# Turning the experts' rows with DMA transposes of 16-bit halves in place of TensorE transposes

## The chip, the core and the metric

The kernel runs on one core of a Trainium2 chip. A core has a matrix engine (TensorE, PE in the profile), a vector engine (VectorE, DVE), a scalar engine (ScalarE, ACT), a general engine (GpSimd, POOL) and an engine that only issues transfers (SyncE, SP). Each works through its own queue of instructions in order and waits for the others by semaphores. Transfers run on 16 DMA engines; they are issued from SP's queue (plain transfers here) or GpSimd's (those with a list of row indices). Tensors lie in SBUF with 128 partitions; TensorE writes to PSUM[...]. The metric is the time of one execution on the device, in microseconds (us), less being better.

## The reference, cut to what matters

```python
x = x + L0_xattn(layernorm(x), ctx)      # correlation of sequences, top 12 shifts
x = x + L0_ffn(layernorm(x))             # 8 experts, 256 tokens each
x = x + L1_xattn(layernorm(x), ctx)      # 16-head attention
x = x + L1_ffn(layernorm(x))

def L1_ffn(h):                           # h: 2048 tokens x 256
    probs = softmax(h @ gate_W.T)        # 8 experts, each token goes to its best two
    gates = top2(probs)
    y_e = (silu(h @ w1[e]) * (h @ w3[e])) @ w2[e]          # 256 -> 1024 -> 256
    shared = mean over 8 narrow shared experts of the same form
    return 0.5 * shared + 0.5 * sum_e gates[:, e] * y_e
```

Everything is in float32. The change lies in the last part, the mixture of experts of the second layer. Its 8 narrow shared experts are handled as one of width 1024, so that it has the size of a routed expert.

## The kernel before, in words

The order of every engine's work is the order of the program: `tc.manual_schedule` (line 1256) leaves each engine's instructions as they are written. What follows from 395 us on is the expert stage.

*Routing.* Each token's row (256 values, 8 gates and its token number, 265 in all) lies in the tile HP. GpSimd scatters the rows, 128 at a time, into a table Td in HBM in which every expert has its own stretch of rows (`send`, line 2887; 32 transfers, each waiting for the one before, the last at 427.14 us). The first 512 rows of an expert are handled in its block; the few beyond that go to "slots" of 32 rows, worked on beside blocks 2 to 6 (`slots`, line 3598), with their own weight loads (`load_slots`) from SP's queue.

*Blocks.* The loop over b (line 3796) has 11 blocks of 512 rows: 0 and 1 are the shared expert on the second and third quarter of the tokens, 2 to 9 are the routed experts 0 to 7, 10 is the shared expert on the last quarter. Block b first runs the up unit (b, 0), then the down unit of block b - 1, then the up units (b, 1) to (b, 3). An up unit computes two 128-wide stretches of the hidden layer; a down unit maps all 1024 back to 256.

*Units.* Each unit is a 2 x 2 block product by seven multiplications (Winograd's form). Its operands are quarters and their sums, the sums being made beforehand by DVE: of the weights (`UpWeights.steps`, `DownWeights.steps`), of the rows (`Rows.steps`, which writes tile T and one quarter of the rows in place) and of the activations (`act_sums`). `run_unit` (line 3407) writes out the order: the seven products, reads of PSUM by ACT and DVE between them, and the end of the unit before (`end_open`), whose gate products and sums DVE makes then. It takes lists of further work to be put at four places, called early, amid, late and after. A down unit's products read the four act tiles of its block in the order 0, 1, 2, 3.

*Rows of an expert.* `load_rows` (line 3489) asks on SP for 512 rows from Td, into the one buffer R. TensorE needs them with the 256 features on the partitions: `Turned.half` turns four 128 x 128 squares into one PSUM bank and ACT copies them into RT (two buffers). Half 0 runs early and half 1 amid the down unit of block b, for the rows of block b + 1; for expert 0 both run in unit (1, 3). Two small DVE copies take the token numbers (ids) and gates (gts) out of R. Then DVE makes the sums T, late in the same down unit.

*Results.* A routed down unit scales its rows by the gates and GpSimd adds them, in four transfers of 128 rows, to the rows of the output Od in HBM (`add_rows`, line 3517). Each of the four waits until the one before has landed. The slots add four small ones of their own.

*Space.* HP is no longer needed once it is sent, and its first 3072 of 4240 elements per partition hold the sums of the up weights (SW, line 3758). Of X, the first six of 16 tiles hold the sums of the down weights from block 2 on (TW); the last four (lrows) are stored to Od ahead of the stage and come back in the last block.

Of the kernel before, what the change touches and what calls it, by code (L numbers as in the profile page):

```python
# [9 lines left out]
F32 = mybir.dt.float32  # L10
BF16 = mybir.dt.bfloat16
U32 = mybir.dt.uint32
I32 = mybir.dt.int32
AF = mybir.ActivationFunctionType
ALU = mybir.AluOpType
# [4 lines left out]
P = 128  # L20
LN_EPS = 1e-5
CAP1 = 576
FIRST = 512
# [1063 lines left out]
def fast_path(  # L1087
# [33 lines left out]
    nc = tc.nc  # L1121
    B, S, D = x.shape
    T = B * S
    NT = T // P
    KC = D // P
    TPB = S // P
    E = L0_ffn_w1.shape[0]
# [22 lines left out]
    X = res.tile([P, NT, D], F32, name="X")  # L1150
# [3 lines left out]
    ROW = D + E + 1  # L1154
# [13 lines left out]
    ident = const.tile([P, P], F32, name="ident")  # L1168
# [93 lines left out]
    pm = l0.enter_context(tc.tile_pool(name="pm", bufs=2))  # L1262
# [34 lines left out]
    for dst, src, i in (  # L1297
# [12 lines left out]
        out=bqd.rearrange("o (b c) -> (o b) c", b=B),  # L1310
        in_=L0_xattn_bq.partition_broadcast(B),
    )
    nc.scalar.dma_start(
        out=WZ[:, :, DH : 2 * DH],
        in_=L0_xattn_Wq.rearrange("(kc p) c -> p kc c", p=P),
# [267 lines left out]
    for h in range(TPB):  # L1583
# [36 lines left out]
        out=tri,  # L1620
        in_=tri,
# [26 lines left out]
    for sign, base in ((1, 1), (-1, 16)):  # L1648
        nc.gpsimd.affine_select(
            out=rows_f,  # L1650
            in_=rows_f,
# [33 lines left out]
    for r in range(2):  # L1685
        (nc.sync if r == 0 else nc.scalar).dma_start(
            out=Gd[0, 0 : S * W2].rearrange(
                "(tt p r w) -> p tt r w", p=P, r=2, w=S
            )[:, :, r, :],
            in_=G,  # L1690
# [4 lines left out]
        out=DG,  # L1695
        in_=Gd[0, :].rearrange("(tt p w) -> p tt w", p=P, w=W2 + 1)[:, :, 1 : S + 1],
# [53 lines left out]
    for tt in range(2):  # L1750
# [3 lines left out]
    rest = pa.tile([P, S], F32, name="rest")  # L1754
# [4 lines left out]
        out=rest, in_to_replace=top[:, 0, :], in_values=pcorr, imm_value=-3.0e38  # L1759
# [16 lines left out]
        out=Wd[:, 0:W2].rearrange("o (r s) -> o r s", r=2),  # L1776
        in_=wrow.unsqueeze(1).to_broadcast([P, 2, S]),
# [4 lines left out]
        out=CW,  # L1782
        in_=bass.AP(wd.tensor, wd.offset + P - 1, [[WD - 1, P], [P, 2], [1, S]]),
# [186 lines left out]
    sums = pa.tile([P, NT, 2], F32, name="sums")  # L1970
# [50 lines left out]
    halves = [slice(m * S, (m + 1) * S) for m in range(2)]  # L2021
# [7 lines left out]
    b = order_b  # L2029
# [101 lines left out]
    def load_row(e):  # L2131
# [14 lines left out]
        out=Yd.rearrange("(c p) d -> p c d", p=P),  # L2146
        in_=blank[:, 0:D].unsqueeze(1).to_broadcast([P, NT, D]),
# [300 lines left out]
    for e in range(E - 1):  # L2448
        if e == 5:

            wpv = L1_xattn_Wp.rearrange("(c g m d) n -> m g d c n", c=NB, g=4, m=2)
            for m in range(2):
                for g in range(4):
# [3 lines left out]
                        out=bvc[r0 : r0 + DH, :],  # L2457
                        in_=bkv[:, 1, :].rearrange("(c g m) d -> m g d c", c=NB, g=4)[m, g],
# [70 lines left out]
    ps_m = banks.enter_context(tc.tile_pool(name="ps_m", bufs=3, space=PSUM))  # L2529
# [436 lines left out]
    for b in range(B):  # L2966
        for c in range(NB):
# [55 lines left out]
            if prev is None:  # L3023
# [12 lines left out]
                HP = pg1.tile([P, NT, ROW], F32, name="HP")  # L3036
# [20 lines left out]
    FULL = FIRST // P  # L3057
# [7 lines left out]
    lrows = slice(LAST * (TB // P), NT)  # L3065
    HT2 = TB // 2
    HF = F // 2
# [17 lines left out]
    class UpWeights:  # L3085


        def __init__(self, wab, sums, s1=None):
            self.sums = sums
            self.raw = {  # L3090
                (h, kc): wab[:, :, kc, h * HF : (h + 1) * HF]
                for h in range(2)
                for kc in range(KC)
            }
            self.part = {
                A11: self.raw[0, 0],
                A12: self.raw[0, 1],
                A22: self.raw[1, 1],
                S1: self.raw[1, 0] if s1 is None else s1,
                S3: sums[:, :, 0],  # L3100
                S2: sums[:, :, 1],
                S4: sums[:, :, 2],
            }
# [120 lines left out]
    class Up(Unit):  # L3224
        n = TB
# [56 lines left out]
    class Down(Unit):  # L3282
        n = HT2
# [123 lines left out]
    def run_unit(u, early=(), amid=(), late=(), after=()):  # L3407

        before = open_unit[0]
        u.mm(u.a, A11, "b11", True)  # L3410
        u.seed()
        if before is not None:
            before.silu_2()
        u.mm(u.e, S1, "t1", True)
        u.read_p5()
        end_open()
        for do in early:
            do()
        u.mm(u.a, S2, "t2")
        u.read_u2()  # L3420
        u.mm(u.b, A12, "b21")
        for do in amid:
            do()
        u.mm(u.e, S4, "b22")
        u.read_c12()
        for do in late:
            do()
        u.mm(u.a, S3, "t3")
        u.read_c22()
        for do in after:  # L3430
            do()
        open_unit[0] = u
# [56 lines left out]
    def load_rows(e):  # L3489
        R = pe2.tile([P, FULL, ROW], F32, tag="R", name="R", bufs=1)  # L3490
        nc.sync.dma_start(
            out=R,
            in_=Td[e * CAP1 : e * CAP1 + FIRST, :].rearrange("(r p) w -> p r w", p=P),
        )
        return R

    class Turned:


        def __init__(self, e, R):  # L3500
            self.e, self.R = e, R
            self.RT = pe2.tile([P, KC, FIRST], F32, tag="RT", name="RT")
            self.ids = pe2.tile([P, FULL], U32, tag="ids", name="ids", bufs=3)
            self.gates = pe2.tile([P, FULL], F32, tag="gts", name="gts", bufs=3)

        def half(self, kc):
            pt = ps_m.tile([P, FULL, P], F32, tag="pm", name="pt")
            for r in range(FULL):
                nc.tensor.transpose(
                    pt[:, r, :], self.R[:, r, kc * P : (kc + 1) * P], ident  # L3510
                )
            nc.scalar.copy(self.RT[:, kc, :], pt.rearrange("p r q -> p (r q)"))
            if kc == 0:
                nc.vector.tensor_copy(self.ids, self.R[:, :, ROW - 1])
                nc.vector.tensor_copy(self.gates, self.R[:, :, D + self.e])

    def add_rows(Y, ids):
        nc.gpsimd.indirect_dma_start(  # L3518
# [164 lines left out]
    pe2 = ctx.enter_context(tc.tile_pool(name="pe2", bufs=2))  # L3683
# [63 lines left out]
    ps_m = ctx.enter_context(tc.tile_pool(name="ps_m", bufs=1, space=PSUM))  # L3747
# [20 lines left out]
    ups, downs, xs_, acts, Rs = {0: shared, 1: shared}, {}, {}, {}, {}  # L3768
    downs[0] = downs[1] = shared_down
    xs_[0], xs_[1], xs_[NBLK - 1] = rows[1], rows[2], rows[LAST]  # L3770
    turned = {}

    def up_unit(b, k):
        u = Up(ups[b], xs_[b], k, acts.setdefault(b, []))
        u.with_sums = b < NBLK - 1
        return u
# [19 lines left out]
    for b in range(NBLK):  # L3796


        n = b + 1
        rest = ups[b].steps(P, HF) if b >= 2 else []  # L3800
        run_unit(up_unit(b, 0), after=rest[:2])
        if b == 0:
            Rs[2] = load_rows(0)
        if b >= 2 and b - 1 < E:
            W_up[b - 1] = load_up(w1p, b - 1)
        halves = []
        if 2 <= n < NBLK - 1:
            t = turned[n] = Turned(n - 2, Rs.pop(n))
            xs_[n] = Rows(t.RT)
            halves = [lambda: t.half(0), lambda: t.half(1)]  # L3810
        sums = xs_[n].steps() if n < NBLK else []
        if b > 0:
            late = b == 1
            run_unit(
                down_unit(b - 1),
                early=([] if late else halves[:1]) + rest[2:],
                amid=[] if late else halves[1:],
                late=[] if late else sums,
            )
        if 2 <= b < E:  # L3820
            Rs[b + 2] = load_rows(b)
        for k in range(1, NK):
            early, amid, after = [], [], []
            if k == 1 and 2 <= n < NBLK:
                ups[n] = UpWeights(WS[0] if n == NBLK - 1 else W_up.pop(n - 2), SW)
                after = ups[n].steps(0, P)
            if 2 <= b < NBLK - 1:
                if k == 2:
                    downs[b] = DownWeights(W_down.pop(b - 2), TW)
                    after = downs[b].steps()[:2]  # L3830
                if k == 3:
                    after = downs[b].steps()[2:]
            if b == 0:
                after = ([assign_slots], sums, shared_down.steps())[k - 1]
            if b == 1 and k == 3:
                early, amid, after = halves[:1], halves[1:], sums
            run_unit(up_unit(b, k), early, amid, after=after)
            if k == 1:
                if b >= 2 and b - 1 < E:
                    W_down[b - 1] = load_down(w1p, b - 1)  # L3840
                if b == 1:
                    flags()
                    experts = slot_experts()
                if b == 2:
                    beside = slots()
                if b == NBLK - 1:
                    nc.sync.dma_start(out=X[:, lrows, :], in_=odv[:, lrows, :])
                    nc.sync.dma_start(
                        out=out.rearrange("b s d -> (b s) d")[0 : LAST * TB, :],
                        in_=Od[0 : LAST * TB, :],  # L3850
                    )
            if beside is not None and (b, k) != (2, 2):
                next(beside, None)
        if b == 1:
            Rs[3] = load_rows(1)
    last_down(WS[1], acts.pop(NBLK - 1))
    order.close()

# [51 lines left out]
```

## Time and profile before

| | |
|---|---|
| median of 3 runs | 831.76 us (830.33 to 832.37) |
| the profiled execution | 830.43 us, its span 828.7 us |
| granted TensorE clock | 0.998 |
| TensorE busy | 806.3 us, 97% of the span |
| DVE, ACT, GpSimd busy | 522.3, 348.7 and 216.8 us |
| DMA | 105.4 MB; engines busy 35.0% by SP's and 7.2% by GpSimd's queue |
| a block with slots / without | 41.0 / 37.6 us |

The profile is of one execution. Rows give the line, engine, operation and tiles (out<-in), their count and durations; a timeline gives start and duration in microseconds from the span's start; "idle before" names what an engine waited for. The durations of matmuls overlap in their pipeline, so that the distance of their starts, not their durations, tells what they cost. Where an engine waits for several things, the profile names the one that came last by its own reckoning.

### The profile page before, as it was taken

The page shows a single profiled execution, that of the slowest core. Times are in us where ns is not written, and L with a number is a line of the kernel's source. Part 1 is how long each engine was busy: PE and PEld are TensorE (multiplying, and loading weights), DVE is VectorE, ACT ScalarE, POOL GpSimd, SP SyncE. Part 2 cuts the span into 40 slices and gives each one's busy share as a digit, 9 for nine tenths or more (in the row PEclk, how much of TensorE's full clock was granted, in tenths as well). Part 3 has the DMA queues.
Part 4 walks back from the last instruction along what each step waited for, and adds up shares of the span by engine and source line. Part 5 has one row for each costly group of instructions (what it writes and reads, how often), then busy time and mean ns, then how long its engine had stood idle before and what let it go on. Part 6 is the DMA issues. An engine that isn't in the chain of part 4 may idle for free.

```text
span 828.7 us, 13872 instructions
## 1 busy us (share of the span) xinstructions
PE 806.3 (97%) x5188; PEld 636.2 (77%) x5188; DVE 522.3 (63%) x1470; ACT 348.7 (42%) x720; POOL 216.8 (26%) x293
## 2 busy tenths in 40 slices
PE   7999999999999999999999999999999999999997
PEld 6546787778745555557898989797979798999996
DVE  6377877440456586555775866767676758586731
ACT  4344454324377777431333233333333433443430
POOL 6251131230125455452330000202111232112020
PEclk9999999999999999999999999999999999999999
DMA  8395567942160000042120474656575754311023
GB/s 261 97 277 177 178 207 224 297 158 84 51 178 15 14 1 28 34 168 89 67 67 26 142 242 135 190 168 187 172 199 161 201 167 122 105 13 20 8 35 124
DMA packets 87316, 105.40 MB, mean 127 GB/s; under 512 B 9000, under 2 KB 77832, under 8 KB 87208
## 3 DMA queue, kind: packets, MB, share of 16 engines
q1 hardware_dynamic: 78568, 91.10, 35.0%
q0 software_dynamic: 7920, 13.02, 7.2%
q8 instruction: 43, 0.70, 0.4%
q10 hardware_dynamic: 752, 0.30, 0.1%
q14 instruction: 33, 0.27, 0.1%
HBM read 80.61 MB, written 25.37 MB: 128 GB/s over the span
## 4 chain that ended last, share of the span: by engine, by line
PE 88%; DMA 5%; DVE 3%; POOL 2%; ACT 1%; issue 1%; ACTq 0%; SPq 0%; DVEq 0%; POOLq 0%
PE a L3234 18%; PE e L3234 9%; PE a L3293 9%; PE py L2389 6%; PE ph L2372 5%; PE B L3234 5%; PE e L3293 4%; PE p L2652 4%; PE py L3439 3%; PE pv L2667 3%; PE B L3293 2%; PE pp L2718 2%; DMA R<-NMd,ids 2%; PE pgt L3196 2%; PE pp L2619 2%; PE pu L3196 2%
## 5 line engine op out<-in xcount | busy, mean ns | idle before, releaser
L3518 POOL DMA_INDIRECT Od<-Y,ids x32 | 51.6, 1612 | 300.5 <-DVE T L3083 184.0
L3222 ACT COPY B<-a 128x512 f32<-128x512 f32 (+1 forms) x54 | 28.6, 531 | 180.5 <-PE a L3234 142.6
L2660 ACT ACTIVATE ex<-p,scale 128x512 f32<-128x512 f32 x128 | 77.2, 689 | 27.5 <-PE p L2652 26.3
L3234 PE MATMUL a<-T,HP 128*128 128x256 f32 x288 | 73.9, 379 | 0.0
L3083 DVE TENSOR_TENSOR cc<-e,s 128x512 f32<-128x512 f32 x44 | 30.4, 691 | 58.0 <-PE e L3234 58.0
L3234 PE MATMUL a<-RT,wab 128*128 128x256 f32 x256 | 66.6, 383 | 0.0
L3083 DVE TENSOR_TENSOR act<-act 128x256 f32<-128x256 f32 (+1 forms) x120 | 61.4, 512 | 2.7
L2372 PE MATMUL ph<-RT,w 128*128 128x256 f32 x256 | 61.7, 389 | 0.8 <-ACT RT L2359 0.7
L2389 PE MATMUL py<-w,A 128*128 128x256 f32 x256 | 61.6, 388 | 0.0
L3234 PEld LDWEIGHTS a<-T,HP 128*128 128x128 f32 x288 | 54.0, 190 | 7.0
L3234 PEld LDWEIGHTS a<-RT,wab 128*128 128x128 f32 x256 | 46.4, 190 | 8.4 <-issue 1.6
L2381 ACT ACTIVATE A<-ph,b1c 128x256 f32<-128x256 f32 x64 | 30.0, 472 | 53.9 <-PE ph L2372 50.6
L2372 PEld LDWEIGHTS ph<-RT,w 128*128 128x128 f32 x256 | 45.3, 190 | 8.9 <-ACT A L2381 1.1
L2389 PEld LDWEIGHTS py<-w,A 128*128 128x128 f32 x256 | 46.6, 190 | 6.4
L2892 POOL DMA_INDIRECT Td<-HP,to x32 | 32.9, 1030 | 56.9 <-DMA Td<-HP,to 51.6
L2652 PE MATMUL p<-QM,KT 32*128 32x512 f32 x256 | 43.4, 640 | 0.4 <-DVE QM L2633 0.4
L3083 DVE TENSOR_TENSOR act<-act,cc 128x512 f32<-128x512 f32 x44 | 30.4, 691 | 17.6 <-ACT act L3268 17.1
L2399 POOL DMA_INDIRECT Yd<-Y,ids x16 | 15.7, 984 | 81.9 <-DVE Y L2398 49.0
L2667 PE MATMUL pv<-ex,VA 128*32 128x256 f32 x512 | 34.5, 385 | 0.2 <-DVE ov L2677 0.2
L3249 ACT COPY s<-a 128x512 f32<-128x512 f32 x44 | 25.7, 585 | 20.4 <-PE a L3234 20.4
L2667 PEld LDWEIGHTS pv<-ex,VA 128*32 128x32 f32 x512 | 13.5, 109 | 27.0 <-issue 11.7
L3234 PE MATMUL e<-T,wab 128*128 128x256 f32 x128 | 33.0, 380 | 0.3 <-DVE T L3083 0.3
(525 smaller groups left out, 1745.0 us busy)
## 6 DMA issues: line engine op xcount, KB each, us to landing
w<-in_L_ffn_w_dram SPq DMA_DIRECT2D x16, 1024.0 KB, 6.0
wab<-in_L_ffn_w_e_dram SPq DMA_DIRECT2D x16, 1024.0 KB, 4.9
wc<-in_L_ffn_w_e_dram SPq DMA_DIRECT2D x8, 1024.0 KB, 5.4
sab<-in_L_ffn_w_e_dram SPq DMA_DIRECT2D x32, 256.0 KB, 2.9
R<-Td SPq DMA_DIRECT2D x8, 530.0 KB, 3.7
sc<-in_L_ffn_w_e_dram SPq DMA_DIRECT2D x16, 256.0 KB, 2.8
Td<-blank SPq DMA_DIRECT2D x2, 1590.0 KB, 10.2
X<-in_x_dram SPq DMA_DIRECT2D x4, 512.0 KB, 5.3
```

What stands on the lines that cost most here:

```text
L2372: nc.tensor.matmul(ph, w1[:, kc, f * P : (f + 1) * P], RT[:, kc, :], start=(kc == 0), stop=(kc == KC - 1),)
L2381: nc.scalar.activation(A[:, f, :], ph, AF.Gelu_apprx_tanh, bias=b1c[:, e, f : f + 1])
L2389: nc.tensor.matmul(py, A[:, f, r * P : (r + 1) * P], w2[:, f, :], start=(f == 0), stop=(f == NF - 1),)
L2652: nc.tensor.matmul(ps[g].rearrange("p m q -> p (m q)"), KT[rows, c, k0 : k0 + P], QM[b][rows, c].rearrange("p m q -> p (m q)"), start=True ...
L2660: nc.scalar.activation(e4[:, g], ps[g], AF.Exp, scale=scale)
L2667: nc.tensor.matmul(pvs[b, c][32 * g : 32 * g + 32, m, :], VA[:, b * TPB + kt, 8 * c + 2 * g + m, :], ex[b, c, kt][:, g, m, :], start=(kt = ...
L2892: nc.gpsimd.indirect_dma_start(out=Td, out_offset=bass.IndirectOffsetOnAxis(ap=to[g][:, k, j : j + 1], axis=0), in_=HP[:, GT * g + j, :], ...
L3083: eng.tensor_tensor(out, a, b, op)
L3196: nc.tensor.matmul(ps, wab[:, m, kc, fs], xs[kc], start=(kc == 0), stop=(kc == KC - 1),)
L3234: nc.tensor.matmul(ps[:, m * HT2 : (m + 1) * HT2], self.w.get(m, left, self.k), self.x.part[right], start=start and m == 0, stop=True, ski ...
L3293: nc.tensor.matmul(ps[:, qs], self.acts[k][:, left, qs], self.w.get(right, k), start=start and i == 0 and k == 0, stop=(k == NK - 1), skip ...
L3518: nc.gpsimd.indirect_dma_start(out=Od, out_offset=bass.IndirectOffsetOnAxis(ap=ids, axis=0), in_=Y, in_offset=None, compute_op=ALU.add,)
```

## The change

The transposes of the routed experts' rows leave TensorE. For the rows of an expert, GpSimd copies the 32-bit values out of R as 16-bit halves into the last four tiles of X, all low halves of a row before all high ones. Four DMA transposes from SP's queue, one for each 128 rows, turn them into a stretch of HP behind the weight sums. Two GpSimd copies (`join`) put the halves together into RT. ACT's copies from PSUM are gone too.

The places change with it. `Turned` (with the ids and gates, the split and the four transposes) now runs at the end of block b, after unit (b, 3), for the rows of block b + 2, from block 0 on. `join` runs in block b + 1, after its first up unit. The sums T stay where they were: late in the down unit, or after unit (1, 3) for expert 0. The load of R for block b + 2 is asked for in block b after the down unit, in block 1 too, where it was at the end of the block; for expert 0 it stays in block 0 after the first unit.

```diff
+U16 = mybir.dt.uint16
...
     class Turned:
         def __init__(self, e, R):
-            self.e, self.R = e, R
-            self.RT = pe2.tile([P, KC, FIRST], F32, tag="RT", name="RT")
             self.ids = pe2.tile([P, FULL], U32, tag="ids", name="ids", bufs=3)
             self.gates = pe2.tile([P, FULL], F32, tag="gts", name="gts", bufs=3)
-
-        def half(self, kc):
-            pt = ps_m.tile([P, FULL, P], F32, tag="pm", name="pt")
+            nc.vector.tensor_copy(self.ids, R[:, :, ROW - 1])
+            nc.vector.tensor_copy(self.gates, R[:, :, D + e])
+            parts = X[:, lrows, :].bitcast(U16).rearrange("p r (t d) -> p r t d", t=2)
+            nc.gpsimd.tensor_copy(
+                parts.rearrange("p r t d -> p r d t"),
+                R[:, :, 0:D].bitcast(U16).rearrange("p r (d t) -> p r d t", t=2),
+            )
+            self.turned = (
+                HP.rearrange("p n r -> p (n r)")[:, 2 * 3 * HF : 2 * 3 * HF + KC * FIRST]
+                .bitcast(U16)
+                .rearrange("p (c q) -> p c q", q=FIRST)
+            )
             for r in range(FULL):
-                nc.tensor.transpose(
-                    pt[:, r, :], self.R[:, r, kc * P : (kc + 1) * P], ident
-                )
-            nc.scalar.copy(self.RT[:, kc, :], pt.rearrange("p r q -> p (r q)"))
-            if kc == 0:
-                nc.vector.tensor_copy(self.ids, self.R[:, :, ROW - 1])
-                nc.vector.tensor_copy(self.gates, self.R[:, :, D + self.e])
+                nc.sync.dma_start_transpose(
+                    out=self.turned[:, :, r * P : (r + 1) * P],
+                    in_=parts[:, r].rearrange("p t d -> p (t d)"),
+                )
+
+        def join(self):
+            self.RT = pe2.tile([P, KC, FIRST], F32, tag="RT", name="RT")
+            for kc in range(KC):
+                nc.gpsimd.tensor_copy(
+                    self.RT[:, kc, :].bitcast(U16).rearrange("p (q t) -> p q t", t=2),
+                    self.turned[:, kc : kc + 3 : 2, :].rearrange("p t q -> p q t"),
+                )
+            return Rows(self.RT)
...
-        halves = []
         if 2 <= n < NBLK - 1:
-            t = turned[n] = Turned(n - 2, Rs.pop(n))
-            xs_[n] = Rows(t.RT)
-            halves = [lambda: t.half(0), lambda: t.half(1)]
+            xs_[n] = turned[n].join()
...
-                early=([] if late else halves[:1]) + rest[2:],
-                amid=[] if late else halves[1:],
+                early=rest[2:],
...
-        if 2 <= b < E:
+        if 1 <= b < E:
             Rs[b + 2] = load_rows(b)
...
             if b == 1 and k == 3:
-                early, amid, after = halves[:1], halves[1:], sums
-            run_unit(up_unit(b, k), early, amid, after=after)
+                after = sums
+            run_unit(up_unit(b, k), after=after)
+            if k == 3 and b < E:
+                turned[b + 2] = Turned(b, Rs.pop(b + 2))
...
-        if b == 1:
-            Rs[3] = load_rows(1)
```

More of the change, by code (lines that the diff above doesn't have):

```diff
@@ L3815, in fast_path @@
                 down_unit(b - 1),
-                early=([] if late else halves[:1]) + rest[2:],
-                amid=[] if late else halves[1:],
+                early=rest[2:],
                 late=[] if late else sums,
             )
-        if 2 <= b < E:
+        if 1 <= b < E:
             Rs[b + 2] = load_rows(b)
         for k in range(1, NK):
-            early, amid, after = [], [], []
+            after = []
             if k == 1 and 2 <= n < NBLK:
```

## The prediction

> **What bounds the kernel now.** I read the page's busy times and its chain first. TensorE works through 97% of the span, at a granted clock of 0.998 in the list of cores:
>
> ```profile
> PE 806.3 (97%) x5188; PEld 636.2 (77%) x5188; DVE 522.3 (63%) x1470; ACT 348.7 (42%) x720; POOL 216.8 (26%) x293
> PE 88%; DMA 5%; DVE 3%; POOL 2%; ACT 1%; issue 1%; ACTq 0%; SPq 0%; DVEq 0%; POOLq 0%
> ```
>
> Then the chain in order of time over the expert stage and the answer for tile R. The transposes are on the chain, four at a time:
>
> ```profile
> 452.69 0.44 PE pt L3509 x4
> 453.13 0.86 PE a L3234 x4
> ...
> 472.03 0.44 PE pt L3509 x4
> L3509 PE MATMUL pt<-ident,R x64: 272/273/273, 452.5 to 711.7; 128*128 128x128 f32 x64
> ```
>
> A transpose is recorded at 0.273 us, but four hold TensorE for 0.44 us. From 395.7 to 822 us TensorE waits for nothing worth naming (one 0.3 us wait for DVE at 458).
>
> Third, the timelines of SP, DVE and PE where the changed order first bites, and the waits of SP:
>
> ```profile
> 422.74 0.68 DVE L3083 TENSOR_TENSOR act<-act,cc 128x512 f32<-128x512 f32 x1
> 423.34 0.41 DVE L3083 TENSOR_TENSOR act<-act,B 128x256 f32<-128x256 f32 x1
> 425.32 1.95 PE L3293 MATMUL a<-wc_-1_2739,act 128*128 128x128 f32 x16
> 429.73 0.36 SPq L3491 DMA_DIRECT2D R<-Td  x1
> SPq L3491 <- DMA Td<-HP,to: 33.6, 1, 33.6
> GB/s 57 0 0 0 0 0 0 0 0 0 0 42 106 78 106 155 85 191 339 389 382 375 375 382 410 417 283 156 254 0 0 0 0 0 0 0 0 0 0 0
> ```
>
> The last line is the DMA view of 429 to 435 us in 40 slices of 0.15 us: R of the first expert, issued at 429.73 when the scatters to Td have landed, is in by 29 slices, at 433.4 us.
>
> Fourth, the deadline of a turned tile in a later block (period 41.0 us) and GpSimd's queue:
>
> ```profile
> 553.83 0.75 DVE L3083 TENSOR_TENSOR T<-RT 128x256 f32<-128x256 f32 x2
> 555.42 0.60 DVE L3362 SCALAR_TENSOR_TENSOR Y<-a,gts,Y 128x128 f32<-128x128 f32 x2
> 556.42 1.95 PE L3293 MATMUL a<-wc,act 128*128 128x128 f32 x16
> 572.83 1.55 POOL L3518 DMA_INDIRECT Od<-Y,ids  x1 [6.26 <-ACT act L3259]
> 673.69 1.85 POOL L3518 DMA_INDIRECT Od<-Ys,ids_s  x1 [1.69 <-DMA Od<-Ys,ids_s]
> 676.81 0.75 DVE L3083 TENSOR_TENSOR T<-RT 128x256 f32<-128x256 f32 x2
> L1597 POOL COPY WK<-wkv_in 128x512 f32<-128x512 f32 x1 | 0.7, 711 | 0.0
> L1561 POOL COPY rexp<-R 128x256 f32<-128x256 f32 x1 | 0.4, 393 | 0.1
> ```
>
> DVE's sums T wait for the turned rows, and behind them stands the read (L3362) that TensorE needs 0.4 us after its end (556.02 to 556.42). So T may start 0.4 us late; beyond that TensorE stops, microsecond for microsecond.
>
> [...] two DVE scalings beside a GpSimd addition took 2.39 us at 232.29 where such a pair takes 0.73 us; but DVE's two-input X<-X,yg kept its 0.68 us at 260.49 beside GpSimd's scaling, and that GpSimd pair took 2.73 us, 2.44 us where no such DVE operation ran.
>
> **The change, part by part.**
>
> *Removed:* 16 groups of four transposes, 16 x 0.44 = 7.0 us, all on the chain. The 16 ACT copies (L3512, 0.585 us each) go too, 9.4 us of an engine with 42%: nothing on the path.
>
> *Moved, first expert:* Turned now runs at the end of block b, two blocks ahead, and starts with two DVE copies from R (ids, gates). In block 0 they stand between the last sum of the shared down weights (ends 422.8) and the gating of unit (0,3) (422.74). R is in at 433.4. DVE therefore stops from 422.8 to 433.4, spends 0.3 us on the copies, and does the two gate products (0.61 + 0.41) by 434.8. Queued behind on DVE is all of act tile 3; the down unit at 425.32 reads acts 0, 1, 2 and then 3, so three matmuls run (1.78/16 = 0.11 us each, to 425.65) and TensorE waits until 434.85: **9.2 us lost**. What follows on DVE (the act sums by 436.7, the c22 read of unit (1,0) by 437.9) is just in time for TensorE's shifted order (second product 436.7, t4 at 438.1). Nothing later gives it back, TensorE being full. Before the change R comes at the same time, but is first read at 452.5; that cover is gone. In block 1 and later R lands long before the copies, which cost nothing.
>
> *Added on GpSimd, per expert:* one copy of 2048 elements, two of 1024. From 711 and 393 ns, an element costs 1.24 ns: 2.6 us and 2 x 1.35. [...] each DVE operation inside stretches a copy by 0.29 us (above). From 2.6 to 6.5 us for either step; I take 4 and 4.
>
> *Added on SP:* four transposes of 128 KB. [...] a tiny transfer (ids_s) takes 1.8 us to land[...]. I take 8 us.
>
> *Is it in time?* From block 3 the split stands on GpSimd behind the four additions to Od of the down unit, which end at 574.4 (572.83 + 1.55) in a block whose successor needs T at 553.83 + 41.03 = 594.9. Less 0.9 for the transposes gone before T, plus 0.4: a window of 20.0 us for split, transposes and join, 4 + 8 + 4 = 16. Hidden, with 4 us to spare. In block 6 four additions from the slots stand between split and join; they end at 675.5, the join at 679.5, T is due at 676.8 - 0.9 + 0.4 = 676.3: **3.2 us lost** (1.9 to 5.7 for joins of 2.7 to 6.5).
>
> *SP's queue:* the transposes wait there for the split, and behind them stand the slots' loads (sab at 563.75, sc at 577.26) and the next up weights (580.0). With the split done at 578 and 5 us of issue, sab goes out by 588, sc by 590, the weights at 591; 5 MB at about 350 GB/s (the slices above reach 375 to 417) from 583 are in by 598 to 600. They are read at 602.8 (the slots' matmul at 561.75 + 41.03) and 603.5 (DVE's sums at 562.47 + 41.03): nothing, with 3 us to spare.
>
> [...] at 433.4 R frees both DVE's copies and GpSimd's split. If GpSimd wins, DVE waits one split more, 4 us; elsewhere DVE is idle 30% of a block. From 0 to 8 us over all; I take 1.
>
> **Sum:** -7.0 + 9.2 + 3.2 + 1.0 = +6.4 us on the profiled execution's span of 828.7, that is 836.8 for its 830.43. The median of the runs is 1.3 us above that execution: **838 us**.
>
> **Rivals.**
> 1. *The cover holds without the later losses (834):* only removal and the first wait, -7.0 + 9.2 = +2.2. [...] Against: the join can't pass the slots' additions on GpSimd.
> 2. *GpSimd and the transposes become the bound (850 to 905):* if split, transposes and join exceed 20 us, five blocks (3 to 7) lose the excess each: 25 us gives +25 more, 863[...]. For it: no row shows a 16-bit copy on GpSimd or a DMA transpose. Against: it needs three prices near their high ends, or slow transposes alone (12 us or more).
> 3. *Faster, 828:* the first wait costs next to nothing because R is there when DVE asks, leaving -7.0 + 3.2. It decides at R's landing: the loss is landing - 424.2, so with the other terms at nothing, 431.2 is the point; R would have to land 2.2 us earlier than it did. Against: its issue is held by the scatters to Td (33.6 us of SP's wait), which the change leaves alone.
>
> **How the numbers follow.** Likeliest case 0.50, 838 (its own range 834.5 to 845); rival 1 0.16; rival 2 0.26; rival 3 0.08. What a measurement can tell from no change is 0.3%, 2.5 us: 829.3 to 834.3. Faster 0.08 is rival 3; within 0.17 is rival 1 and a sliver; slower 0.75. Low end 832: the 0.08 below is rival 3. High end 862: about 0.12 above it, the worse half of rival 2.
>
> **What would show it.** No pt from R, TensorE's busy time down by some 7 us. DVE idle for 10 to 11 us until R lands in 420 to 440, and TensorE stopped for about 9 us from about 425.6 until act: if that is missing, the main step is wrong. T waiting for GpSimd's RT for about 3 us in one block after the slots' additions; if it does so in five blocks, rival 2. Transposes' landing, and the copies' durations against 4, 8 and 4 us. The prediction is wrong above all if the 16-bit steps take far longer than taken here.

## The result, and the profile after

The changed kernel takes 895.12 us in the median of four runs (890.08 to 896.05), against 831.18 us for the kernel before. The ratio is 1.0756, with a 95% interval of 1.0713 to 1.0799. The profiled execution took 895.65 us with a span of 893.9 us, 65.2 us more than the 828.7 us of before. So the forecast had the sign right and the size wrong: 838 us was named, with 862 us as the upper end.

First the page of the changed kernel: the busy times and the chain, then the new group of GpSimd (columns after the bar: busy us, mean ns of one, idle before).

```profile
PE 821.6 (92%) x5124; PEld 643.3 (72%) x5124; DVE 588.5 (66%) x1470; ACT 342.1 (38%) x704; POOL 311.2 (35%) x317
...
PE 71%; DVE 11%; DMA 6%; POOL 5%; issue 4%; ACT 1%; ACTq 0%; SPq 0%; POOLq 0%; DVEq 0%
...
L3509 POOL COPY X<-R 128x2048 uint16<-128x2048 uint16 x8 | 77.3, 9665 | 35.4 <-DMA R<-Td 35.4
```

TensorE's share of the chain falls from 88 to 71%, and DVE's rises from 3 to 11%. The split takes 9.7 us, where I had taken 4 and bounded it at 6.5. DVE's busy time has grown by 66 us although its instructions are as many as before. One group of DVE, before (first fence) and after (second), shows that the same additions have become longer:

```profile
L3083 DVE TENSOR_TENSOR act<-act,cc 128x512 f32<-128x512 f32 x44 | 30.4, 691 | 17.6 <-ACT act L3268 17.1
```

```profile
L3084 DVE TENSOR_TENSOR act<-act,cc 128x512 f32<-128x512 f32 x44 | 49.0, 1113 | 12.0 <-ACT act L3269 11.7
```

The waits of TensorE in the expert stage (in total, times, longest; us), where before there was one of 0.3 us:

```profile
PE a L3294 <- DVE act L3084: 11.6, 1, 11.6
PE a L3235 <- POOL X L3509: 10.9, 2, 5.4
PE pys L3670 <- DVE aT L3666: 10.5, 2, 5.3
PE a L3235 <- DVE cc L3084: 7.1, 1, 7.1
PE a L3235 <- DVE act L3084: 5.3, 2, 3.3
PE e L3294 <- DVE act L3084: 4.1, 1, 4.1
```

With two more, of 0.5 us for DVE's Y and 0.3 us for its T, they add up to 50.3 us. The rest of the 65.2 us is TensorE's own work: its busy time rose by 15.3 us (821.6 for 806.3) although 7.0 us of transposes left it, so the remaining matmuls took about 22 us longer. The sum is 50.0 + 15.3 = 65.3 us. T, which would be late if split, transposes and join were too slow, costs TensorE 0.3 us, as before.

The stops of more than 1 us are one for R and one for each of the eight splits. That holds for the two put down to GpSimd's X as well. In the first of them DVE's act<-act,cc is held beside the split; TensorE goes on at 667.02, 0.7 us after the split's end (666.33) but right behind DVE's act<-act,a (666.52 to 666.93), which reads tile a, where the waiting matmuls write, and stood in DVE's queue behind the held addition:

```profile
656.51 9.82 POOL L3509 COPY X<-R 128x2048 uint16<-128x2048 uint16 x1
656.59 9.67 DVE L3084 TENSOR_TENSOR act<-act,cc 128x512 f32<-128x512 f32 x1
...
667.02 1.19 PE L3235 MATMUL a<-RT,wab 128*128 128x256 f32 x2 [5.44 <-POOL X L3509]
```

One block shows how the stops arise. First DVE's work in question before the change, then the timeline after, 606 to 620 us (start, duration, engine, line, what it waited for):

```profile
570.58 1.28 DVE L3083 TENSOR_TENSOR X<-wc 128x512 f32<-128x512 f32 x2
```

```profile
606.80 10.49 DVE L3084 TENSOR_TENSOR X<-wc 128x512 f32<-128x512 f32 x2
607.54 9.81 POOL L3509 COPY X<-R 128x2048 uint16<-128x2048 uint16 x1
...
617.67 1.94 PE L3670 MATMUL pys<-sc,aT 128*32 128x256 f32 x16 [5.26 <-DVE aT L3666]
...
619.54 2.08 PE L3235 MATMUL a<-RT,wab 128*128 128x256 f32 x4
```

DVE's pair of additions X<-wc took 1.28 us before. Here it takes 10.49 us and ends with GpSimd's split (617.29 and 617.35). TensorE has work for some 4.5 us of the split (9.8 less 5.3), then stops for 5.3 us until DVE has written aT, its next piece of work. Afterwards four matmuls take 2.08 us in place of 1.03. The granted clock is 0.50 from 617.6 to 621.6 us, 0.66 from there to 624 and 1.00 from 624 to 630. It is 0.93 in each 50 us from 550 to 800 us; in the kernel before it was 1.00 in each up to 750 us.

The first expert's block, 427 to 450 us, is the stop that was forecast, and a second one behind it:

```profile
436.48 0.17 DVE L3506 CAST ids<-R 128x4 uint32<-128x4 f32 x1 [12.71 <-DMA R<-Td]
436.78 9.62 POOL L3509 COPY X<-R 128x2048 uint16<-128x2048 uint16 x1 [5.49 <-DMA R<-Td]
...
437.89 9.36 DVE L3084 TENSOR_TENSOR act<-act 128x256 f32<-128x256 f32 x3
438.03 3.78 PE L3294 MATMUL a<-wc_-1_2739,act 128*128 128x128 f32 x16 [11.60 <-DVE act L3084]
...
446.85 2.50 PE L3294 MATMUL e<-TS,act 128*128 128x128 f32 x10 [4.05 <-DVE act L3084]
```

R was asked for at 432.84. DVE waits for it (12.7 us), TensorE for DVE (11.6 us). Then the split starts, holds DVE's act sums until 447, and TensorE stops once more.

### The profile page after: what moved, and what is told of

Read it like the earlier page. It is cut to its first block, busy times and chain, and to the rows that moved or that the text cites. A ratio compares the mean times of both kernels' runs of the same rounds, so it can differ in the third digit from the quotient of the medians.

```text
span 893.9 us, 13820 instructions
## 1 busy us (share of the span) xinstructions
PE 821.6 (92%) x5124; PEld 643.3 (72%) x5124; DVE 588.5 (66%) x1470; ACT 342.1 (38%) x704; POOL 311.2 (35%) x317
## 4 chain that ended last, share of the span: by engine, by line
PE 71%; DVE 11%; DMA 6%; POOL 5%; issue 4%; ACT 1%; ACTq 0%; SPq 0%; POOLq 0%; DVEq 0%
PE a L3235 13%; PE a L3294 8%; PE py L2390 6%; PE e L3235 6%; PE ph L2373 6%; PE e L3294 4%; PE p L2653 4%; DVE act L3084 3%; PE B L3235 3%; PE pv L2668 3%; DVE X L3084 2%; POOL X L3509 2%; PE B L3294 2%; PE pp L2719 2%; PE pgt L3197 2%
## 5 line engine op out<-in xcount | busy, mean ns | idle before, releaser
L3235 PE MATMUL a<-RT,wab 128*128 128x256 f32 x256 | 73.4, 413 | 19.9 <-POOL X L3509 10.9
L3509 POOL COPY X<-R 128x2048 uint16<-128x2048 uint16 x8 | 77.3, 9665 | 35.4 <-DMA R<-Td 35.4
L3084 DVE TENSOR_TENSOR act<-act 128x256 f32<-128x256 f32 (+1 forms) x120 | 84.5, 704 | 2.7
L3235 PEld LDWEIGHTS a<-RT,wab 128*128 128x128 f32 x256 | 50.5, 208 | 31.7 <-POOL X L3509 11.8
L3084 DVE TENSOR_TENSOR act<-act,cc 128x512 f32<-128x512 f32 x44 | 49.0, 1113 | 12.0 <-ACT act L3269 11.7
L3527 POOL COPY RT<-HP 128x1024 uint16<-128x1024 uint16 x16 | 20.7, 1353 | 54.5 <-PE a L3235 27.9
L3235 PE MATMUL e<-T,wab 128*128 128x256 f32 x128 | 37.4, 419 | 0.3 <-DVE T L3084 0.3
L3269 ACT ACTIVATE act<-cc 128x512 f32<-128x512 f32 x44 | 27.9, 634 | 18.0 <-DVE cc L3084 18.0
```

The lines of the kernel that those rows point to most:

```text
L3084: eng.tensor_tensor(out, a, b, op)
L3235: nc.tensor.matmul(ps[:, m * HT2 : (m + 1) * HT2], self.w.get(m, left, self.k), self.x.part[right], start=start and m == 0, stop=True, ski ...
L3509: nc.gpsimd.tensor_copy(parts.rearrange("p r t d -> p r d t"), R[:, :, 0:D].bitcast(U16).rearrange("p r (d t) -> p r d t", t=2),)
```

## The experiments

**Theory A**, formed from this profile: GpSimd's split is slow because of the order in which it walks the halves (low and high half of each value in turn, which are written 512 bytes apart), and while it runs it holds DVE's two-input operations. The stops follow from its length. Its rivals put the loss elsewhere: in the new work as such (copies on GpSimd, transposes in the queues) whatever the copy's length; or in the first wait for R and what it delays. The expectations say for each theory what it expects.

### The split in another order

The same copy with its loops exchanged: all low halves of a row first, side by side in what is written, 4 bytes apart in what is read.

```diff
             nc.gpsimd.tensor_copy(
-                parts.rearrange("p r t d -> p r d t"),
-                R[:, :, 0:D].bitcast(U16).rearrange("p r (d t) -> p r d t", t=2),
+                parts,
+                R[:, :, 0:D].bitcast(U16).rearrange("p r (d t) -> p r t d", t=2),
             )
```

> The change with one edit: the split on GpSimd walks its elements half by half, so that it writes 16-bit values side by side and reads them 4 bytes apart, where it read side by side and wrote low and high halves 512 bytes apart in turn. Same engine, elements, places and waits. Theory A (the split costs 9.7 us for its form of writing and holds VectorE's two-input operations for as long as it runs): the split takes 2.6 to 3 us like two joins of 1.35 us, TensorE's waits of 5.3 us in blocks 3 to 7 go, and what is left is the first wait for R (about 12 us and its clock): 838 to 846 us. Theory B (the transposes, the loads behind them on SP and late joins cost the time): within 10 us of the change, 885 or more. Theory C (the first wait for R is most of it): within 15 us of the change, 880 or more.

Measured: 842.28 us (840.21 to 844.4), ratio 1.0155 (1.0132 to 1.0177). The split's group and the longest waits of TensorE in this kernel:

```profile
L3509 POOL COPY X<-R 128x2048 uint16<-128x2048 uint16 x8 | 18.4, 2301 | 36.6 <-DMA R<-Td 36.6
```

```profile
PE a L3294 <- DVE act L3084: 9.7, 1, 9.7
PE a L3294 <- DVE Y L3363: 2.9, 1, 2.9
```

One exchange of loops takes the split from 9.7 to 2.3 us and the kernel from 895 to 842 us. DVE's act<-act,cc is back at 691 ns. What is left is what the prediction had named: the first wait (9.7 us for 9.2) and the join behind the slots' additions (2.9 us for 3.2); the other waits come to 0.5 us. The rival that blames the new work as such falls: copy, transposes and joins are all still there.

### The first wait moved, the split as it was

```diff
-            nc.vector.tensor_copy(self.ids, R[:, :, ROW - 1])
-            nc.vector.tensor_copy(self.gates, R[:, :, D + e])
+            self.e, self.R = e, R
...
         def join(self):
+            nc.vector.tensor_copy(self.ids, self.R[:, :, ROW - 1])
+            nc.vector.tensor_copy(self.gates, self.R[:, :, D + self.e])
```

> The change with one edit: the two VectorE copies of token numbers and gates move from the end of block b into the join in block b + 1, so that VectorE doesn't wait for R of the first expert at the end of block 0. The split keeps its form. Theory A: only the first wait goes (11.6 us on TensorE); the split of the first expert then holds VectorE at another place, so 8 to 15 us less than the change: 880 to 888. Theory C: most of the loss goes, below 850.

Measured: 893.04 us (two runs), ratio 1.0758 (1.0728 to 1.0787): no gain that shows, against the 880 to 888 us that theory A expected. In the join of block 1 the copies still stand ahead of the down unit that DVE must read next, and R is not in yet. The longest such wait of TensorE:

```profile
PE a L3294 <- DVE X L3317: 8.4, 1, 8.4
```

The wait was moved by one unit and not taken away (8.4 and 3.0 us, for 11.6 and 4.1 in the changed kernel), and the split's holds remain. So this run says nothing of what the first wait costs; the run with the first wait alone, further down, does.

### Both edits

The two diffs above together.

> Both edits: the split writes side by side, and VectorE's copies of numbers and gates stand in the join. Theory A: nothing of the loss is left but the join behind the slots' additions in block 7 (0 to 4 us), and the transposes' 7.0 us are gained: 823 to 829 us, faster than the kernel before. Theory B: 870 or more.

Measured: 835.62 us (832.51 to 842.53, eight runs), ratio 1.0081 (1.0051 to 1.0111). It missed the expected 823 to 829, because of two waits. One is that for R, as in the run above (4.9 us in two parts). The other is in GpSimd's and DVE's timelines:

```profile
678.35 1.33 POOL L3535 DMA_INDIRECT Od<-Ys,ids_s  x1 [5.16 <-DMA wab<-in_L_ffn_w_e_dram]
679.23 2.69 POOL L3528 COPY RT<-HP 128x1024 uint16<-128x1024 uint16 x2
...
680.87 1.68 DVE L3084 TENSOR_TENSOR T<-RT 128x256 f32<-128x256 f32 x2 [2.91 <-POOL RT L3528]
```

The join waits for the last of the slots' additions, T for the join, and TensorE for what stands behind T: 3.3 us.

### The first wait alone, in the kernel before

TensorE keeps the transposes; only the two small copies of the first expert move to the end of block 0.

```diff
             run_unit(up_unit(b, k), early, amid, after=after)
+            if b == 0 and k == 3:
+                turned[2] = Turned(0, Rs.pop(2))
+                turned[2].take()        # ids and gates of the first expert
```

> The kernel before, TensorE's transposes kept, with one edit: for the first expert alone the two VectorE copies of token numbers and gates are made at the end of block 0 in place of block 1. Nothing on GpSimd or SP is changed. The prediction's first step alone: VectorE waits for R from 422.8 to about 433.5 us and TensorE stops for 9 to 10 us at the first down unit and starts again at a lower clock: 9 to 12 us more than before, 840 to 843. If R's wait were covered: 831.

Measured: 846.25 us (844.95 to 847.51) against 832.96, ratio 1.0159 (1.0134 to 1.0184), +13.3 us, above the 840 to 843 us expected. From its timeline:

```profile
440.20 3.58 PE L3293 MATMUL a<-wc_-1_2739,act 128*128 128x128 f32 x16 [11.83 <-DVE act L3083]
```

TensorE stands for 11.8 us, where 9 to 10 were expected, after DVE's 12.85 us for R, and its busy time over the whole kernel is 3.1 us above that of before: sixteen matmuls that took 1.95 us (at 425.32 before) take 3.58 us after the stop. Two copies of four elements cost 13 us, because of what they wait for.

### The split alone, in the kernel before

Six slow splits on GpSimd at the ends of blocks 2 to 7; nothing reads what they write, and TensorE still turns the rows.

```diff
+            if k == 3 and 2 <= b < E:
+                nc.gpsimd.tensor_copy(
+                    X[:, lrows, :].bitcast(U16).rearrange("p r (t d) -> p r d t", t=2),
+                    Rs[b + 2][:, :, 0:D].bitcast(U16).rearrange("p r (d t) -> p r d t", t=2),
+                )
```

> The kernel before, with TensorE's transposes kept, and with the split alone added on GpSimd at the end of blocks 2 to 7, in the form of the change; nothing reads what it writes. No DMA transposes, no joins, no moved loads or copies. Theory A: each of the six splits takes 9 to 10 us, VectorE's operation beside it 5 to 10 us, and TensorE stops 2 to 6 us in each block and runs at a lower clock after it: 855 to 880 us. Theories B and C: 832 us, since nothing waits for the split.

Measured: 876.59 us (two runs), ratio 1.0559 (1.0528 to 1.0591), +46 us or 7.7 us for each split. The two largest waits of TensorE (a third is 0.2 us, for T):

```profile
PE a L3235 <- DVE cc L3084: 27.0, 4, 7.0
PE a L3235 <- DVE act L3084: 8.3, 2, 6.1
```

There are six stops for six copies of 9.7 us, 35.3 us in all, and matmuls 14.4 us longer (820.7 us busy for 806.3). With neither transposes by DMA nor joins nor the first wait, most of the loss is here. The first wait falls as the main cause: its own run gave 13 us of the 64.

### The split on ScalarE, in its slow order

To part the order of writing from the engine: ACT makes the same copy (`nc.scalar.copy` for `nc.gpsimd.tensor_copy`), the joins stay on GpSimd, and the copies from R stand after the down unit of block 1 and later ahead of the sums T.

> The change with the split in its own form (low and high halves written in turn, 512 bytes apart), but made by ScalarE; the joins stay on GpSimd. VectorE's copies of numbers and gates stand ahead of the sums T (for the first expert after the down unit of block 1), so that the first wait is gone. Theory A[...]: VectorE's operations keep 0.4 to 0.7 us beside the split, and if ScalarE takes 2 to 3 us for it, 823 to 832 us; if ScalarE is as slow as GpSimd for this form (9 us), its own late copies stop TensorE and the time is 850 or more, VectorE's durations unchanged all the same. If it is not the engine but the writing itself that blocks, VectorE's operations are stretched here too.

Measured: 901.29 us (898.68 to 904.65), ratio 1.0827 (1.0792 to 1.0862). ACT's and DVE's groups, and then the longest waits of TensorE:

```profile
L3508 ACT COPY X<-R 128x2048 uint16<-128x2048 uint16 x8 | 74.2, 9280 | 18.6 <-DMA R<-Td 18.6
...
L3084 DVE TENSOR_TENSOR act<-act 128x256 f32<-128x256 f32 (+1 forms) x120 | 61.4, 512 | 2.7
```

```profile
PE a L3235 <- ACT B L3223: 54.6, 8, 23.8
```

The order is slow on ACT too, 9.3 us. But DVE's act sums have their 512 ns of before again (704 ns in the changed kernel), so the hold on DVE belongs to GpSimd. The kernel loses as much in another way: what TensorE needs of ACT (B) stands behind the copy, and once, for 23.8 us, behind ACT's wait for R.

### Prices beside each other

Behind the last block of the kernel before, GpSimd copies 2048 elements (1024 in the last form) between tiles no longer needed, in five forms: once without and once beside two DVE additions of 512 elements with both inputs in SBUF, which take 0.69 us each otherwise. The very first copy, of the slow form, had nothing to wait for and ran ahead, at 804.24 beside the last block; it took 9.81 us. The added work makes this kernel's time no measure of anything else.

```diff
+    for to_, from_ in forms:
+        nc.gpsimd.tensor_copy(to_, from_)
...
+        nc.gpsimd.tensor_copy(to_, from_)
+        tt(seen, HT[:, 1, 0:TB], HT[:, 1, TB : 2 * TB], ADD)
+        tt(seen, HT[:, 1, 0:TB], HT[:, 1, TB : 2 * TB], SUB)
```

> The kernel before, with GpSimd copies on dead tiles added after its last matmul, each form twice: 2048 16-bit values in the change's split form; the same with the writes side by side; the same plain; 2048 32-bit values plain; 1024 16-bit values in the join's form. Beside the second copy of each form VectorE makes two additions of 512 values with both inputs in SBUF (0.69 us alone). The time itself means nothing. Theory A: 9.7, about 2.2, about 2.2, 2.6 and 1.3 us; the first addition ends with the copy beside it, whatever its form. If only the form that writes far apart blocks VectorE, the additions beside the others take 0.69 us.

Measured, GpSimd's and DVE's timeline; the slow form, the halves side by side, and the plain 16-bit copy without additions beside it:

```profile
832.50 9.67 DVE L3084 TENSOR_TENSOR seen<-HT 128x512 f32<-128x512 f32 x2
832.53 9.73 POOL L3878 COPY HP<-HT 128x2048 uint16<-128x2048 uint16 x1 [18.48 <-DVE seen L3877]
...
844.44 2.98 DVE L3084 TENSOR_TENSOR seen<-HT 128x512 f32<-128x512 f32 x2
844.47 2.42 POOL L3878 COPY HP<-HT 128x2048 uint16<-128x2048 uint16 x1 [0.25 <-DVE seen L3877]
846.95 2.23 POOL L3875 COPY HP<-HT 128x2048 uint16<-128x2048 uint16 x1
```

The plain copy reads in the same order as the slow one, side by side, and differs in the writes alone: 2.23 us for 9.7. So it is the order of the writes that is slow.

Beside a copy of 9.73 us the two additions take 9.67, beside one of 2.42 us they take 2.98. The pair ends 0.1 us ahead of the slow copy's end and 0.5 us behind the end of the other. The two are one record, so whether one or both are held isn't shown. The forms with plain 16-bit values (2.42 us) and with 32-bit values (2.42 us) hold just as long as they run (2.99 and 2.98 us for the pair), and the join's form (1.67 us) too (2.25 us). So in these five forms the length of the pair follows the length of the copy, to within 0.6 us, whatever the type or stride. Which of the two came first the trace doesn't tell, as their recorded starts lie 0.03 us apart.

### Can the idea be made to pay?

Three edits together: the side-by-side order; the copies of ids and gates after the down unit of block 1 and later just ahead of the sums T; and the slots' last step one unit further on, so that its additions no longer stand ahead of the join.

```diff
-            if beside is not None and (b, k) != (2, 2):
+            if beside is not None and (b, k) not in ((2, 2), (6, 3)):
                 next(beside, None)
```

> Three edits to the change: the split on GpSimd writes side by side; VectorE's copies of numbers and gates stand ahead of the sums T (for the first expert after the down unit of block 1); the slots' last step, whose additions stood ahead of a join on GpSimd, comes one unit later, in block 7. Theory A: nothing of TensorE's waits is left but fractions of a microsecond; against the kernel before, 7.0 us of transposes are gained: 822 to 826 us, faster than both kernels. If splits and joins still cost VectorE too much: 828 or more.

Measured: 842.87 us (842.16 to 844.63), ratio 1.0119 (1.0099 to 1.014), a miss. The additions now stand ahead of the split of block 7 instead. Its timeline:

```profile
714.66 1.33 POOL L3537 DMA_INDIRECT Od<-Ys,ids_s  x1 [1.89 <-DMA Od<-Ys,ids_s]
...
728.82 3.78 PE L3294 MATMUL a<-wc,act 128*128 128x128 f32 x16 [9.75 <-DVE Y L3363]
```

The split follows at 715.54, the join 6.58 us after its end at 724.47, and T behind that; all come too late, and TensorE stops for 9.75 us. In the next kernel the slots' last step is made in block 8, behind the last split and join (the steps at (7, 1), (7, 2) and (7, 3) are left out too).

> As the three edits before (split side by side on GpSimd, VectorE's copies late), but with the slots' last step in block 8, behind the last join, where one unit later it had only moved its four additions ahead of a split and so stopped TensorE for 9.7 us. Theory A: TensorE's long waits are gone; what GpSimd's splits and joins still hold of VectorE (about 5 us a block) costs 1 to 3 us in all; against 7.0 us of transposes gained: 3 to 6 us faster than the kernel before (0.993 to 0.996 of it). If those holds eat the gain: within 0.3% of it or slower.

Measured: 831.23 us (829.55 to 834.92, 14 runs), ratio 0.9988 (0.9972 to 1.0003): as fast as before, no faster. TensorE still stops for 3.2 us over all, 2.4 us of it in three places for DVE's cc. cc itself takes 0.69 us, as before; other additions of DVE are longer than before in the mean (act<-act,cc 0.76 us for 0.69, act<-act 0.60 for 0.51).

Last, the GpSimd copies go to ACT, which lost 16 copies of 0.585 us by the change. The split is in the side-by-side order at the end of the block; the joins stand early and amid the down unit, where ACT's copies from PSUM stood before; the first expert's split and transposes stand behind the down unit of block 1, its joins in unit (1, 3). DVE's copies of ids and gates come late, as in the three edits.

```diff
-            nc.gpsimd.tensor_copy(
-                parts.rearrange("p r t d -> p r d t"),
-                R[:, :, 0:D].bitcast(U16).rearrange("p r (d t) -> p r d t", t=2),
+            nc.scalar.copy(
+                parts,
+                R[:, :, 0:D].bitcast(U16).rearrange("p r (d t) -> p r t d", t=2),
             )
...
+        def join(self, kc):
+            nc.scalar.copy(
+                self.RT[:, kc, :].bitcast(U16).rearrange("p (q t) -> p q t", t=2),
+                self.turned[:, kc : kc + 3 : 2, :].rearrange("p t q -> p q t"),
+            )
...
-                early=rest[2:],
+                early=halves[:1] + rest[2:],
+                amid=halves[1:],
...
-            if k == 3 and b < E:
+            if k == 3 and 1 <= b < E:
                 turned[b + 2] = Turned(b, Rs.pop(b + 2))
```

> The change with split and joins on ScalarE in place of GpSimd, the split writing side by side, the two halves of the join where the kernel before had ScalarE's copies out of PSUM, VectorE's copies late, and for the first expert split and transposes after the down unit of block 1, the join in unit (1,3). GpSimd has nothing to do with the turning[...]; the slots stay as they were. Theory A: TensorE gains the 7.0 us whole if ScalarE's split takes 2 to 3 us (a 9.3 us split cost 4 to 5 us of waiting, so 5 us were covered): 6 to 7 us faster than the kernel before (0.991 to 0.993 of it). If the DMA transposes or the loads behind them on SP cost something by themselves, it shows here: less than 4 us faster.

Measured: 828.36 us (825.4 to 829.41, eight runs) against 832.51, ratio 0.9942 (0.9921 to 0.9963): faster than both kernels, if by a little less than the 6 to 7 us expected. The split's group, and the only wait of TensorE:

```profile
L3508 ACT COPY X<-R 128x2048 uint16<-128x2048 uint16 x8 | 15.3, 1912 | 6.2 <-DMA R<-Td 6.2
```

```profile
PE e L3235 <- DVE T L3084: 0.3, 1, 0.3
```

From the first matmul of the expert stage to the end of the span, this execution takes 826.3 - 400.5 = 425.8 us, the one before 828.7 - 395.7 = 433.0: 7.2 us less. The ratio makes it 4.8 us (3.1 to 6.6). By the same measure the kernel with the slots' step last is 3.0 us shorter (828.8 - 398.8 = 430.0), where its ratio makes it 1.0. In the profiled executions the stage begins anywhere from 394.4 to 400.5 us, though nothing ahead of it was edited; whether the edits shift that beginning on average isn't settled.

## Why the prediction was right or wrong

**Removed, 7.0 us: right by the trace.** In the profiled execution the stage of the last kernel is 7.2 us shorter, with no new stop. The whole kernel gains 4.8 us; what lies between is the beginning of the stage, which stays open.

**The split's price, taken at 4 us, bounded at 6.5: the step that failed.** Measured 9.7 us. I carried 1.24 ns an element over from copies whose elements lie side by side; the 4 us, and the 6.5 as the upper end, were estimates that no row of the kernel before shows. The writes set it: halves written 512 bytes apart in turn cost 4.7 ns each, side by side 1.1. The prediction had named 16-bit steps that take far longer as what would make it wrong above all.

**DVE beside GpSimd's copies, taken at 1 us, bounded at 8: failed with it.** The stops other than the first expert's come to 34 us, and with the slower matmuls after them to most of the 65; the split alone cost 46 us in six blocks. Two things went wrong. I charged one hold in one place, where R frees DVE and GpSimd together, though the split stands in the middle of DVE's two-input work in every block. And I let one row speak against the hold: X<-X,yg at 260.49 overlaps the first of GpSimd's two scalings by some 0.3 us (an estimate from its start at 259.54 and 1.22 us for one, half of 2.44), so it could have shown little of a hold; the pair's extra 0.29 us may be one, of GpSimd by DVE, which this row alone doesn't show. The additions here do show the hold: the pair of 1.28 us took 10.49 beside the split. The two terms belong together: in the block shown TensorE has cover for about 4.5 us of a hold, so a split of 2.3 us costs next to nothing (in the first experiment DVE's X<-wc took 1.31 us in the mean, for 0.68 before, and TensorE waited 0.2 us for DVE's cc). The least cover of the eight is 2.7 us (9.8 less the stop of 7.1). An estimate from these: a split of 4 us would have cost 1.3 us in that block and nothing in the others, near my 1 us. With the split short the whole sum comes near, too: the first experiment took 842 us where 838 was named.

**First wait, 9.2 us: right in mechanism, too small.** DVE's two copies wait for R, act tile 3 behind them, TensorE for that. The stop is 11.6 us, mainly because R was asked for at 432.84 and not at 429.73 (the stage began 1 us later, the scatters took the rest), 11.8 us in the kernel with this step alone, and 9.7 in the first experiment. The three matmuls that I let run ahead of the stop wait as well. Not in the sum at all: the slower matmuls after the stop (3.58 us for 1.95 in the kernel with this step alone, which took 13.3 us more).

**Join behind the slots' additions, 3.2 us: right.** It is hidden in the changed kernel, whose blocks have become longer (0.5 us), and shows as 2.9 and 3.3 us once the split is short.

**Transposes 8 us, joins 4 us: too high.** Both were estimates; the kernel before has no DMA transpose and no 16-bit copy on GpSimd. Where the join waits for the transposes it begins 6.5 to 6.8 us after the split's end; in the block shown it is 6.9 us (617.35 to 624.28), but there the profile names TensorE as what it waited for. The two joins take 2.2 to 3.0 us. With the slow split that is 9.8 + 6.9 + 2.4 = 19.1 us in the block shown, inside the window of 20.0. No run here turns 32-bit values by DMA, so what the halves are needed for is not shown.

**SP's queue, nothing: right.** The four transposes took 5.1 us of the queue in the block shown, for my estimate of 5. No wait of TensorE names a weight's transfer.

**Rival 2** (850 to 905) holds the measured time, but not by its mechanism, so that is luck: T is not late. The engine that bounds these stretches is GpSimd, through what it does to DVE. Rival 3 falls, as R lands later and not earlier; rival 1 is the prediction without its small losses and falls with it.

## What to carry to other kernels

Price a copy by the order of its writes as well as its reads (9.7 us for halves written 512 bytes apart in turn, 2.2 for the plain copy with the same reads), and see whether exchanging its loops gives the same result. Before putting work on GpSimd, ask what DVE does at that moment: if it adds tiles in SBUF, then in these runs the length of each GpSimd copy came on top, less the cover that the bounding engine had (5.3 us of stop for a copy of 9.8 us in the block shown). And count a stop of several microseconds on TensorE higher than its length: 11.8 us of stop cost 13.3 us in the run with the first wait alone.

## What the runs showed of the hardware that was not expected

- 16-bit values written 512 bytes apart in turn: 9.7 us on GpSimd and 9.3 us on ACT for 2048 elements a partition (4.7 and 4.5 ns each), against 1.9 to 2.5 and 1.9 us side by side. Values read 1 or 2 KB apart and written side by side, the join's form, cost 1.3 ns on GpSimd in the changed kernel and 1.6 ns in the run of prices, where a plain 16-bit copy of twice the length cost 1.1 ns; on ACT they cost 1.1 ns.
- In the changed kernel, four DMA transposes of 128 x 512 16-bit values take 5.1 us of SP's queue in the block shown, 1.3 us each, and the joins that wait for them begin 6.5 to 6.8 us after the split's end.
- After the stops of 5.2 to 11.8 us shown here the next group of matmuls takes 1.8 to 2.0 times as long (3.58 us for 1.95, 2.08 for 1.03): with 50 us of stops the matmuls themselves lost about 22 us, with 35 us about 14, with 12 us about 3.
